# Output products of six experts by seven products of halves instead of eight

## The chip, the cores and the metric

The kernel runs on one NeuronCore of a Trainium2 chip. A core has TensorE (PE, matrix products into the banks of PSUM), VectorE (DVE, elementwise work), ScalarE (ACT, elementwise functions), GpSimd (POOL) and SyncE (SP, which here only issues DMA transfers); each engine works through its own instruction stream, and semaphores order them. PEld in a profile is TensorE's load of the stationary operand, which overlaps its matmuls. The metric is device time in microseconds. Before the change it is 1541.7 us (median of 3 runs, 1541.43 to 1544.1).

## The reference

All arithmetic is float32. Input x is 8 sequences of 256 tokens with 512 features, so 2048 tokens. Two layers follow each other; each has a recurrent attention block (WKV) and a feed-forward block. The feed-forward block of layer 0 is a gated MLP with a Walsh-Hadamard transform; the one of layer 1, which the change touches, is a mixture of eight experts:

```
x = x + tanh(g_xattn[0]) * WKV0(layernorm(x), ctx)
x = x + tanh(g_ffn[0])   * (fwht(silu(n @ W1.T) * (n @ W3.T)) @ W2.T)     # n = layernorm(x)
x = x + tanh(g_xattn[1]) * WKV1(layernorm(x), ctx)
x = x + tanh(g_ffn[1])   * moe(layernorm(x))

def moe(x):                                    # 8 experts, 512 -> 1024 -> 512, two per token
    mult, sel = route(x @ gate_w.T)            # sparsemixer: two experts and two weights per token
    combine = sum over the two of mult * one_hot(sel)
    act = silu(x @ w1[e].T) * (x @ w3[e].T)    # hidden values, 1024 per token
    y[e] = act @ w2[e].T                       # output product, 512 per token
    return sum over e of combine[:, e] * y[e]
```

## The kernel before

**Stages.** The first 880 us or so compute the attention blocks and layer 0's MLP, and send each token's normalised row, with its number and weights, into a queue in DRAM for each of its two experts (`dispatch`, L589). Then come the experts. `EARLY = (6, 7)` are taken first, partly while the last tokens are still being routed; then experts 0 to 5 follow in order (`order`, L1288). The change concerns these six.

**Two parts per expert.** `PARTS` (L40) cuts an expert's tokens in a first part of 256 and a second of up to 336. The second part runs only if the expert has more than 256 tokens: its work stands in `tc.If(needed > 0)` (L1089). For each part, `prepare` (L872) loads the rows of the queue (L893, on SP's queue) and turns them by transposes on TensorE (L865), so that features lie on partitions; `old_rows` (L901) gathers the tokens' present rows of the output by an indirect DMA of POOL into tiles g; `weigh` (L1073) adds weight times y to g; `new_rows` (L910) scatters g back. These transfers go in POOL's queue, and each waits for the one before, because all touch the output.

**First parts** are computed by `compute` (L920). Hidden values come in KC = 8 units of 128, each for all 256 tokens: `hidden` (L718) does four matmuls with W1 and four with W3 (L729, 256 columns), then ScalarE's tanh (L733) and two VectorE operations (L734, L735). Behind unit k follow the output matmuls of unit k-1, one for each block of 128 tokens, 512 columns wide (`add`, L926). So a first part has 2 x 8 of these, and the last ones end it. Between the units a generator of background work, `bg`, is advanced by n = 2 steps (L938): preparing the next parts, `sum_tokens` (L975) and `sum_weights` (L954).

**Second parts** of every expert but 6 are computed by `compute_paired` (L988). There the hidden products already are done by seven products of halves instead of eight (Strassen's scheme in Winograd's form): the features and the hidden units of a weight matrix are each halved, and so are the features and the tokens of the token matrix (HALF = 168). `sum_weights` and `last_sum` (L970) make the sums of the weights' quarters, `sum_tokens` those of the tokens. In each of four rounds k, the products go into three PSUM tiles pa, pb, pc (L1006), VectorE adds them up (L1023 to L1055), and gating gives hidden units k and k+4. The output matmuls of a round are kept in a list `late` and put in between later products by `put` (L1037), for three blocks (128, 128 and 80 tokens), again 8 matmuls of 512 columns each. In the last part of all, `leave` is given: there they come block by block at the end, and each block is weighed and stored as soon as it is done. On TensorE this order is kept as written (`manual_schedule`, L1091).

**Order of work otherwise.** In the expert stage the framework's scheduler orders each engine's instructions by their place in the program and by when their operands and buffers are ready; the order is then fixed for the run. Tiles of one tag share a number of buffers: v4 (4 KB per partition; weights, weight sums, turned tokens) has 35 (L84), u2 16, h1 (256 columns) 17; PSUM has three banks for hidden products (`ps_gl`), three for outputs (`ps_o`) and two for transposes. A new tile waits until a buffer is free. An expert's weights are 12 tiles of 512 KB (8 of W1 and W3, 4 of W2), all loaded from SP's queue by `load_expert` (L846).

**The main loop** (L1304) loads the next expert ahead of a part, then runs the part with its background work:

```
early_load = i or e == order[len(EARLY)]          # L1311
...
if i == 0:
    bg = chain(bg, sum_tokens(f"{e}_1"), sum_weights(e))   # L1320
...
part(e, i, bg, 2, needed, at == len(todo) - 1)    # L1324
```

So the next expert's load stands, in program order, ahead of the second part; for the first of the six, expert 0, it stands ahead of the first part.

Of the kernel before, what the change touches and what calls it, by code (L numbers as in the profile page):

```python
# [8 lines left out]
FP = mybir.dt.float32  # L9
# [8 lines left out]
P = 128  # L18
# [32 lines left out]
def flamingo_kernel(  # L51
# [31 lines left out]
    def v4(name, shape=(P, DC, T)):  # L83
        return work.tile(list(shape), FP, tag="v4", name=name, bufs=35)  # L84
# [19 lines left out]
    def chain(*gens):  # L104
        for gen in gens:
            yield from gen
# [810 lines left out]

    def compute(weights, xq, wt, g, width, name, bg=iter(()), n=0, leave=None):  # L920
        w1, w3, w2 = weights
        blocks = [(b, min(P, width - b * P)) for b in range(len(g))]
        ys = [ps_o.tile([P, D], FP, tag="o", name=f"y_{name}_{b}") for b, _ in blocks]
        ts = []

        def add(k, b, rows):  # L926
            nc.tensor.matmul(  # L927
                ys[b][:rows, :], lhsT=ts[k][:, b * P : b * P + rows], rhs=w2_of(w2, k),
                start=(k == 0), stop=(k == KC - 1),
            )  # L930

        for k in range(KC):
            t = None if width <= T else u2([P, width], f"t_{name}_{k}")
            ts.append(hidden(xq, w1, w3, k, width, f"{name}_{k}", t))
            if k > 0 and leave is None:
                for block in blocks:
                    add(k - 1, *block)
            run(bg, n)  # L938
        for b, rows in blocks:
            for k in range(KC - 1 if leave is None else 0, KC):  # L940
                add(k, b, rows)
            if leave is not None:
                weigh(g[b], ys[b], wt, b, rows)
                leave(b)
        if leave is None:
            for b, rows in blocks:
                weigh(g[b], ys[b], wt, b, rows)

# [37 lines left out]
    def compute_paired(e, tokens, wt, g, name, leave=None):  # L988
        w2 = experts[e][2]
        width = 2 * HALF  # L990
        blocks = [(b, min(P, width - b * P)) for b in range(len(g))]
        ys = [ps_o.tile([P, D], FP, tag="o", name=f"y_{name}_{b}") for b, _ in blocks]
        b11, b21, b22, t1, t2, t3, t4 = tokens
        ts = {}

        def add(k, b, rows):
            nc.tensor.matmul(  # L997
                ys[b][:rows, :], lhsT=ts[k][:, b * P : b * P + rows], rhs=w2_of(w2, k),
                start=(k == 0), stop=(k == KC - 1),
            )  # L1000

        def product(ps, to, k, weights, toks):
            for c in range(2):
                nc.tensor.matmul(  # L1006
                    ps[:, to, :], lhsT=weights[:, c, k * P : (k + 1) * P], rhs=toks[:, c, :],
                    start=(c == 0), stop=(c == 1),
                )

        def twice(t):
            return t.to_broadcast([P, 2, HALF])

        def six(k, n):
            a11, a12, a22, s1, s2, s3, s4 = sums[e][n]
            r = u2([P, 4, HALF], f"h{n}_{name}_{k}")
            ps = ps_gl.tile([P, 3, HALF], FP, tag="gl", name=f"pa{n}_{name}_{k}")
            product(ps, 0, k, a11, b11)
            product(ps, 1, k, a12, b21)
            product(ps, 2, k, s2, t2)  # L1020
            nc.scalar.copy(r[:, 1, :], ps[:, 0, :])

            nc.vector.tensor_tensor(r[:, 0:4:3, :], ps[:, 1:3, :], twice(r[:, 1:2, :]), ALU.add)  # L1023
            yield
            ps = ps_gl.tile([P, 3, HALF], FP, tag="gl", name=f"pb{n}_{name}_{k}")
            product(ps, 0, k, s1, t1)
            product(ps, 1, k, s3, t3)
            product(ps, 2, k, s4, b22)
            nc.vector.tensor_tensor(r[:, 1:3, :], ps[:, 0:2, :], twice(r[:, 3:4, :]), ALU.add)
            nc.vector.tensor_tensor(r[:, 3, :], ps[:, 1, :], r[:, 1, :], ALU.add)  # L1030
            nc.vector.tensor_tensor(r[:, 1, :], ps[:, 2, :], r[:, 1, :], ALU.add)
            yield r


        late = []

        def put(n):  # L1037
            for _ in range(min(n, len(late))):
                add(*late.pop(0))

        for k in range(KC // 2):
            last = k == KC // 2 - 1
            rs = []
            for n in range(2):
                both = six(k, n)
                next(both)
                put(2 * n if not last else 0)
                rs.append(next(both))
            put(2 if not last else 0)
            ps = ps_gl.tile([P, 2, HALF], FP, tag="gl", name=f"pc_{name}_{k}")  # L1050
            for n in range(2):
                product(ps, n, k, sums[e][n][2], t4)
            put(len(late))
            for n in range(2):
                nc.vector.tensor_tensor(rs[n][:, 2, :], ps[:, n, :], rs[n][:, 2, :], ALU.add)  # L1055
            t = u2([P, 4, HALF], f"t_{name}_{k}")
            nc.scalar.activation(t, rs[0], AF.Tanh, scale=0.5)
            nc.vector.scalar_tensor_tensor(rs[0], t, 1.0, rs[0], ALU.add, ALU.mult)
            nc.vector.tensor_tensor(rs[1], rs[0], rs[1], ALU.mult)
            for i, j in enumerate((k, k + 4)):  # L1060
                ts[j] = rs[1][:, 2 * i : 2 * i + 2, :].rearrange("p a t -> p (a t)")
            if leave is None:
                late += [(j, b, rows) for j in (k, k + 4) for b, rows in blocks]
        put(len(late))
        for b, rows in blocks:
            if leave is not None:
                for i in range(KC):
                    add(i // 2 + i % 2 * 4, b, rows)
            weigh(g[b], ys[b], wt, b, rows)
            if leave is not None:  # L1070
                leave(b)

    def weigh(g, y, wt, b, rows):  # L1073
        nc.vector.scalar_tensor_tensor(  # L1074
            g[:rows, :], y[:rows, :], wt[:rows, b : b + 1], g[:rows, :], ALU.mult, ALU.add
        )

    def expert_part(weights, xq, meta, width, name, bg, n, needed=None, last=False):
        who, wt = meta
        blocks = range(-(-width // P))  # L1080
        g = [old_rows(who, b, NT, f"{name}_{b}") for b in blocks]
        if needed is None:
            compute(weights, xq, wt, g, width, name, bg, n)
        else:
            paired = weights in sums
            if paired and weights not in EARLY:
                last_sum(weights)
            done = (lambda b: new_rows(who, b, g[b], NT)) if last else None
            with tc.If(needed > 0):  # L1089
                if paired:  # L1090
                    with tc.manual_schedule(engines={mybir.EngineType.PE}):  # L1091
                        compute_paired(weights, sums[name], wt, g, name, done)
                else:
                    compute(experts[weights], xq, wt, g, width, name, leave=done)
        if not last:
            for b in blocks:
                new_rows(who, b, g[b], NT)
# [120 lines left out]

    def part(e, i, bg, n, needed=None, last=False):
        name = f"{e}_{i}"  # L1220
        expert_part(experts[e] if needed is None else e, parts[name], metas[name], PARTS[i][1], name, bg, n, needed, last)


    n_ps = ps_st.tile([P, NE], FP, tag="st", name="n_all")
# [79 lines left out]
    for at, (e, i) in enumerate(todo):  # L1304
        nxt = order.index(e) + 1

        if nxt == len(EARLY) + 1 and i == 0:
            count_overflow()
            overflow()
        load_next = nxt < NE and order[nxt] not in experts  # L1310
        early_load = i or e == order[len(EARLY)]  # L1311
        if load_next and early_load:
            load_expert(order[nxt])
        needed = None
        if i:
            engines = busy + [mybir.EngineType.Pool] * (at == len(todo) - 1)
            needed = nc.values_load(needs[0:1, e : e + 1], engines=engines, min_val=0, max_val=1)  # L1317
        bg = prepare_on(at)
        if i == 0:
            bg = chain(bg, sum_tokens(f"{e}_1"), sum_weights(e))  # L1320
        elif e == EARLY[0]:

            take(chain(sum_weights(EARLY[1], True), sum_tokens(f"{EARLY[1]}_1")))
        part(e, i, bg, 2, needed, at == len(todo) - 1)  # L1324
        take(bg)

        if load_next and not early_load:
            load_expert(order[nxt])
# [46 lines left out]
```

## Time and profile before

| what | us |
|---|---|
| median of three runs | 1541.7 |
| profiled execution, own time | 1540.96 |
| its span, first to last instruction | 1539.2 |
| TensorE busy (share of the span) | 1488.2 (97%) |
| VectorE busy | 892.5 (58%) |
| ScalarE busy | 285.3 (19%) |
| GpSimd busy | 235.8 (15%) |
| mean granted TensorE clock | 0.984 |

The profile is of one execution; its span leaves out some time before the first and after the last instruction. "Busy" is the time in which an engine works on an instruction; a matmul's end is modelled, so starts are surer than ends. A line such as "L927 PE MATMUL y<-w_e,t" names the code line, the engine, the operation, the tile written and the tiles read; "<-DVE g L1074" after idle time names what ended it. A matmul of float32 operands appears as two TensorE instructions.

### The profile page before, as it was taken

The numbers are of one execution on the slowest core, as the hardware profiler recorded it, in microseconds if no ns is written. First come the engines' busy times: TensorE is split into PE (matmuls) and PEld (weight loads), VectorE is DVE, ScalarE is ACT, GpSimd is POOL, SyncE is SP. The second block draws the span as 40 slices with busy tenths as digits, with TensorE's granted clock in tenths as the row PEclk, the third lists the DMA queues.
The fourth block names the chain that finished last, engine by engine and source line by source line (L and its number), as shares of the span: only waits on it lengthen the run. The fifth ranks groups of instructions, "written<-read, shape, count | busy, mean of one in ns | idle before, by whom it ended". The sixth has DMA issues, their size and how long they took to land. (4 is left out here: it accounts for less than half of the span.)

```text
span 1539.2 us, 18611 instructions
## 1 busy us (share of the span) xinstructions
PE 1488.2 (97%) x7072; PEld 1198.3 (78%) x7072; DVE 892.5 (58%) x1987; ACT 285.3 (19%) x665; POOL 235.8 (15%) x258
## 2 busy tenths in 40 slices
PE   5999999999999999999999799899999999999996
PEld 2988888888888888888877557576877868778693
DVE  6852877978787796976355414353435544355452
ACT  5240313223122322312121100011101111111110
POOL 1100111211121221212112201013101011010110
PEclk9899999999999999999999899999999999999998
DMA  9960001011001101023161305336123151231010
GB/s 335 363 223 14 15 28 42 28 42 42 28 29 41 42 28 44 12 90 117 45 216 49 99 14 182 112 119 217 57 90 126 48 202 52 91 123 33 27 32 17
DMA packets 79494, 135.11 MB, mean 88 GB/s; under 512 B 13084, under 2 KB 26524, under 8 KB 79392
## 3 DMA queue, kind: packets, MB, share of 16 engines
q1 hardware_dynamic: 69280, 108.45, 20.5%
q0 software_dynamic: 8960, 25.25, 4.7%
q8 instruction: 60, 0.98, 0.3%
q14 instruction: 42, 0.34, 0.1%
q10 hardware_dynamic: 1152, 0.09, 0.1%
HBM read 100.05 MB, written 37.90 MB: 90 GB/s over the span
## 5 line engine op out<-in xcount | busy, mean ns | idle before, releaser
L746 PE MATMUL gl_f<-xn,w_a 128*128 128x256 f32 (+1 forms) x1152 | 235.6, 359 | 1.6 <-DVE xn L418 1.6
L746 PE MATMUL gl_f<-xn,w_b 128*128 128x256 f32 (+1 forms) x1152 | 223.9, 356 | 0.0
L746 PEld LDWEIGHTS gl_f<-xn,w_a 128*128 128x128 f32 x1152 | 200.9, 193 | 27.7 <-issue 3.3
L746 PEld LDWEIGHTS gl_f<-xn,w_b 128*128 128x128 f32 x1152 | 199.0, 190 | 23.0
L729 PE MATMUL gl<-q,w_e 128*128 128x256 f32 x768 | 179.4, 386 | 9.6 <-DVEq L1281 6.0
L729 PEld LDWEIGHTS gl<-q,w_e 128*128 128x128 f32 x768 | 146.8, 194 | 45.3 <-issue 27.4
L997 PE MATMUL y<-w_e,h 128*128 128x512 f32 (+1 forms) x288 | 129.5, 592 | 0.0
L911 POOL DMA_INDIRECT out<-g,who_e x40 | 41.7, 1042 | 522.1 <-DVE g L1074 427.9
L818 PE MATMUL o_f<-t_f,w_b 128*128 128x256 f32 x512 | 118.7, 380 | 0.0
L818 PE MATMUL o_f<-t_f,w_a 128*128 128x256 f32 x512 | 117.3, 380 | 0.0
L927 PE MATMUL y<-w_e,t 128*128 128x512 f32 (+1 forms) x240 | 111.0, 592 | 0.0
L818 PEld LDWEIGHTS o_f<-t_f,w_b 128*128 128x128 f32 x512 | 96.2, 190 | 12.5
L818 PEld LDWEIGHTS o_f<-t_f,w_a 128*128 128x128 f32 x512 | 96.2, 190 | 12.5
L753 ACT ACTIVATE t_f<-gl_f 128x256 f32<-128x256 f32 (+1 forms) x144 | 50.1, 360 | 297.3 <-PE gl_f L746 296.8
L755 DVE SCALAR_TENSOR_TENSOR t_f<-t_f,gl_f 128x256 f32<-128x256 f32 (+1 forms) x144 | 53.9, 382 | 80.7 <-ACT t_f L753 80.5
L997 PEld LDWEIGHTS y<-w_e,h 128*128 128x128 f32 (+1 forms) x288 | 49.6, 177 | 54.5 <-issue 54.5
L734 DVE SCALAR_TENSOR_TENSOR t<-t,gl 128x256 f32<-128x256 f32 x48 | 20.2, 421 | 117.4 <-ACT t L733 117.1
L927 PEld LDWEIGHTS y<-w_e,t 128*128 128x128 f32 (+1 forms) x240 | 44.9, 187 | 37.9 <-issue 31.4
L1006 PEld LDWEIGHTS pa<-q,w_e 128*128 128x128 f32 x384 | 57.8, 190 | 8.1 <-issue 7.8
L733 ACT ACTIVATE t<-gl 128x256 f32<-128x256 f32 x48 | 18.5, 385 | 239.0 <-PE gl L729 239.0
L1074 DVE SCALAR_TENSOR_TENSOR g<-y,wt_e,g 128x512 f32<-128x512 f32 (+1 forms) x37 | 27.7, 750 | 60.3 <-PE y L997 44.1
L1006 PE MATMUL pa<-q,w_e 128*128 128x168 f32 x384 | 62.6, 306 | 0.0
(223 smaller groups left out, 2058.6 us busy)
## 6 DMA issues: line engine op xcount, KB each, us to landing
w_e<-in_w1T SPq DMA_DIRECT2D x32, 512.0 KB, 6.6
w_e<-in_w3T SPq DMA_DIRECT2D x32, 512.0 KB, 7.0
w_e<-in_w2T SPq DMA_DIRECT2D x32, 512.0 KB, 11.7
queue<-empty SPq DMA_DIRECT2D x8, 1290.0 KB, 16.5
r<-queue SPq DMA_DIRECT2D x32, 256.0 KB, 4.4
c<-in_ctxT SPq DMA_DIRECT2D x15, 512.0 KB, 3.2
out<-xr SPq DMA_DIRECT2D x16, 256.0 KB, 2.1
x<-in_xT SPq DMA_DIRECT2D x7, 512.0 KB, 3.2
```

The costliest lines, as they stand in the source:

```text
L729: nc.tensor.matmul(ps, lhsT=w13_of(w, c, k), rhs=xn(c)[:, :width], start=(c == 0), stop=(c == DC - 1))
L733: nc.scalar.activation(t, gp, AF.Tanh, scale=0.5)
L734: nc.vector.scalar_tensor_tensor(t, t, 1.0, gp, ALU.add, ALU.mult)
L746: nc.tensor.matmul(ps, lhsT=w13_of(w, c, k), rhs=xn(c)[:, :width], start=(c == 0), stop=(c == DC - 1))
L753: nc.scalar.activation(t, gp, AF.Tanh, scale=0.5)
L755: nc.vector.scalar_tensor_tensor(t, t, 1.0, gp, ALU.add, ALU.mult)
L818: nc.tensor.matmul(o, lhsT=w2_of(w2h[k // KC], k % KC)[:, c * P : (c + 1) * P], rhs=hs[k], start=(k == 0), stop=(k == 2 * KC - 1),)
L911: nc.gpsimd.indirect_dma_start(out=out[:end, :], out_offset=bass.IndirectOffsetOnAxis(ap=who[:, b : b + 1], axis=0), in_=g, in_offset=None ...
L927: nc.tensor.matmul(ys[b][:rows, :], lhsT=ts[k][:, b * P : b * P + rows], rhs=w2_of(w2, k), start=(k == 0), stop=(k == KC - 1),)
L997: nc.tensor.matmul(ys[b][:rows, :], lhsT=ts[k][:, b * P : b * P + rows], rhs=w2_of(w2, k), start=(k == 0), stop=(k == KC - 1),)
L1006: nc.tensor.matmul(ps[:, to, :], lhsT=weights[:, c, k * P : (k + 1) * P], rhs=toks[:, c, :], start=(c == 0), stop=(c == 1),)
L1074: nc.vector.scalar_tensor_tensor(g[:rows, :], y[:rows, :], wt[:rows, b : b + 1], g[:rows, :], ALU.mult, ALU.add)
```

## The change

**Output products of pairs.** A new function, `outputs`, computes y for two blocks of 128 tokens at once. The 1024 hidden units are halved (units 0 to 3, `low`, and 4 to 7, `high`), the 512 outputs are halved (`left`, `right`, HC = 256), and the two blocks of tokens are the third pair of halves. Seven products, each of four accumulating matmuls 256 columns wide, fill the halves of three PSUM banks and one half of a fourth; one ScalarE copy and eight VectorE additions combine them into two SBUF tiles y0 and y1, which are then weighed (the second in two halves). In the last part, each block is scattered as it is done.

**Sums.** `sum_down` makes four sums of quarters of W2 for an expert (eight VectorE operations of 128x512 into four v4 tiles), as the last background work of its first part. `sum_units` makes four sums of hidden units for each k of 0 to 3 (four operations of 128x128 into two h1 tiles), in both parts.

**Where.** First parts of experts 0 to 5 compute their hidden units in the order 0, 4, 1, 5, 2, 6, 3, 7, with no output matmuls in between, and then call `outputs`. Their second parts (`pairs`) do their hidden products without output matmuls in between, then the output matmuls of the third block of 80 tokens as before, then `outputs` for the first two blocks. Experts 6 and 7 are unchanged.

**Around it.** Background work advances by 3 steps per unit instead of 2. Expert 1's load moves from ahead of expert 0's first part to ahead of its second part, like the others. For expert 0 the sums of W1 and W3 come first in the background work.

```
-    def compute(weights, xq, wt, g, width, name, bg=iter(()), n=0, leave=None):
+    def compute(weights, xq, wt, g, width, name, bg=iter(()), n=0, leave=None, e=None):
         w1, w3, w2 = weights
+        if e is not None:
+            hs, ss = {}, {}
+            for k in range(KC // 2):
+                for j in (k, k + KC // 2):
+                    hs[j] = hidden(xq, w1, w3, j, width, f"{name}_{j}")
+                    run(bg, n)
+                ss[k] = sum_units(hs, k, name)
+            return outputs(e, hs, ss, wt, g, name)
...
+    HC = D // 2
+    down = {}
+
+    def sum_down(e):
+        w2 = experts[e][2]
+        t1, t2, t3, t4 = (v4(f"t{i}_2_{e}", (P, 4, HC)) for i in (1, 2, 3, 4))
+        down[e] = t1, t2, t3, t4
+        for i in range(2):
+            ks = slice(2 * i, 2 * i + 2)
+            (b11, b12), (b21, b22) = ((w2[j][:, :, :HC], w2[j][:, :, HC:]) for j in (i, i + 2))
+            for t, a, b in ((t1, b12, b11), (t2, b22, t1[:, ks, :]), (t3, b22, b12), (t4, t2[:, ks, :], b21)):
+                nc.vector.tensor_tensor(t[:, ks, :], a, b, ALU.subtract)
+                yield
+
+    def sum_units(hs, k, name):
+        (a11, a21), (a12, a22) = ((hs[j][:, :P], hs[j][:, P : 2 * P]) for j in (k, k + KC // 2))
+        s1, s2, s3, s4 = (
+            t[:, i, :] for t in (h1(2 * P, f"{n}_{name}_{k}").rearrange("p (i t) -> p i t", i=2) for n in ("sa", "sb"))
+            for i in range(2)
+        )
+        nc.vector.tensor_tensor(s1, a21, a22, ALU.add)
+        nc.vector.tensor_tensor(s2, s1, a11, ALU.subtract)
+        nc.vector.tensor_tensor(s3, a11, a21, ALU.subtract)
+        nc.vector.tensor_tensor(s4, a12, s2, ALU.subtract)
+        return s1, s2, s3, s4
+
+    def outputs(e, hs, ss, wt, g, name, leave=None):
...
+        def product_of(ps, cs, a, b):
+            for k in range(KC // 2):
+                nc.tensor.matmul(ps[:, cs], lhsT=a(k), rhs=b(k), start=(k == 0), stop=(k == KC // 2 - 1))
...
+        u, y0, y1 = (u2([P, D], f"{n}_{name}") for n in ("u", "y0", "y1"))
+        ps = bank("a")
+        product_of(ps, left, unit_of(low, 0), weight_of(low, left))
+        product_of(ps, right, unit_of(high, 0), weight_of(high, left))
+        nc.scalar.copy(u[:, left], ps[:, left])
+        nc.vector.tensor_tensor(y0[:, left], ps[:, right], u[:, left], ALU.add)
+        ps = bank("b")
+        product_of(ps, left, sum_of(2), lambda k: t2[:, k, :])
+        product_of(ps, right, sum_of(1), lambda k: t1[:, k, :])
+        nc.vector.tensor_tensor(u[:, right], ps[:, left], u[:, left], ALU.add)
+        nc.vector.tensor_tensor(y0[:, right], ps[:, right], u[:, right], ALU.add)
+        nc.vector.tensor_tensor(y1[:, right], ps[:, right], u[:, right], ALU.add)
+        ps = bank("c")
+        product_of(ps, left, sum_of(4), weight_of(high, right))
+        product_of(ps, right, sum_of(3), lambda k: t3[:, k, :])
+        nc.vector.tensor_tensor(y0[:, right], ps[:, left], y0[:, right], ALU.add)
+        weigh(g[0], y0, wt, 0, P)
+        if leave is not None:
+            leave(0)
+        nc.vector.tensor_tensor(u[:, left], ps[:, right], u[:, right], ALU.add)
+        nc.vector.tensor_tensor(y1[:, right], ps[:, right], y1[:, right], ALU.add)
+        ps = bank("d")
+        product_of(ps, left, unit_of(high, 1), lambda k: t4[:, k, :])
+        weigh(g[1][:, right], y1[:, right], wt, 1, P)
+        nc.vector.tensor_tensor(y1[:, left], u[:, left], ps[:, left], ALU.subtract)
+        weigh(g[1][:, left], y1[:, left], wt, 1, P)
+        if leave is not None:
+            leave(1)
...
     def compute_paired(e, tokens, wt, g, name, leave=None):
+        pairs = e in down
+        if pairs:
+            blocks = blocks[2:]
...
+        def held(k):
+            return pairs or k == KC // 2 - 1
...
-                put(2 * n if not last else 0)
+                put(2 * n if not held(k) else 0)
...
-            put(len(late))
+            put(len(late) if not pairs else 0)
...
+            if pairs:
+                ss[k] = sum_units(ts, k, name)
+            if leave is None or pairs:
                 late += [(j, b, rows) for j in (k, k + 4) for b, rows in blocks]
         put(len(late))
...
+        if pairs:
+            outputs(e, ts, ss, wt, g, name, leave)
...
-        early_load = i or e == order[len(EARLY)]
+        early_load = i > 0
...
         if i == 0:
-            bg = chain(bg, sum_tokens(f"{e}_1"), sum_weights(e))
+            if e == order[len(EARLY)]:
+                bg = chain(sum_weights(e), bg, sum_tokens(f"{e}_1"), sum_down(e))
+            else:
+                bg = chain(bg, sum_tokens(f"{e}_1"), sum_weights(e), sum_down(e))
...
-        part(e, i, bg, 2, needed, at == len(todo) - 1)
+        part(e, i, bg, 3, needed, at == len(todo) - 1)
```

More of the change, by code (lines that the diff above doesn't have):

```diff
@@ new lines, in outputs, with unit_of, weight_of, sum_of @@
+    def outputs(e, hs, ss, wt, g, name, leave=None):
+        w2 = experts[e][2]
+        t1, t2, t3, t4 = down[e]
+        left, right = slice(0, HC), slice(HC, D)
+        low, high = (lambda k: k), (lambda k: k + KC // 2)
+        def unit_of(half, at):
+            return lambda k: hs[half(k)][:, at * P : (at + 1) * P]
+        def weight_of(half, cs):
+            return lambda k: w2_of(w2, half(k))[:, cs]
+        def sum_of(i):
+            return lambda k: ss[k][i - 1]
+        def product_of(ps, cs, a, b):
+            for k in range(KC // 2):
+                nc.tensor.matmul(ps[:, cs], lhsT=a(k), rhs=b(k), start=(k == 0), stop=(k == KC // 2 - 1))
+        def bank(n):
+            return ps_o.tile([P, D], FP, tag="o", name=f"y{n}_{name}")
+        u, y0, y1 = (u2([P, D], f"{n}_{name}") for n in ("u", "y0", "y1"))
[26 more added lines that the diff above has]
+            leave(1)
@@ L991, in compute_paired @@
         blocks = [(b, min(P, width - b * P)) for b in range(len(g))]
-        ys = [ps_o.tile([P, D], FP, tag="o", name=f"y_{name}_{b}") for b, _ in blocks]
+        pairs = e in down
+        if pairs:
+            blocks = blocks[2:]
+        ys = {b: ps_o.tile([P, D], FP, tag="o", name=f"y_{name}_{b}") for b, _ in blocks}
         b11, b21, b22, t1, t2, t3, t4 = tokens
-        ts = {}
+        ts, ss = {}, {}
         def add(k, b, rows):
@@ L1041, in compute_paired @@
         for k in range(KC // 2):
-            last = k == KC // 2 - 1
             rs = []
@@ L1046, in compute_paired @@
                 next(both)
-                put(2 * n if not last else 0)
+                put(2 * n if not held(k) else 0)
                 rs.append(next(both))
-            put(2 if not last else 0)
+            put(2 if not held(k) else 0)
             ps = ps_gl.tile([P, 2, HALF], FP, tag="gl", name=f"pc_{name}_{k}")
@@ L1061, in compute_paired @@
                 ts[j] = rs[1][:, 2 * i : 2 * i + 2, :].rearrange("p a t -> p (a t)")
-            if leave is None:
+            if pairs:
+                ss[k] = sum_units(ts, k, name)
+            if leave is None or pairs:
                 late += [(j, b, rows) for j in (k, k + 4) for b, rows in blocks]
@@ L1065, in compute_paired @@
         for b, rows in blocks:
-            if leave is not None:
+            if leave is not None and not pairs:
                 for i in range(KC):
@@ L1076, in weigh, with expert_part @@
         )
-    def expert_part(weights, xq, meta, width, name, bg, n, needed=None, last=False):
+    def expert_part(weights, xq, meta, width, name, bg, n, needed=None, last=False, e=None):
         who, wt = meta
@@ L1082, in expert_part @@
         if needed is None:
-            compute(weights, xq, wt, g, width, name, bg, n)
+            compute(weights, xq, wt, g, width, name, bg, n, e=e)
         else:
@@ L1220, in part @@
         name = f"{e}_{i}"
-        expert_part(experts[e] if needed is None else e, parts[name], metas[name], PARTS[i][1], name, bg, n, needed, last)
+        expert_part(experts[e] if needed is None else e, parts[name], metas[name], PARTS[i][1], name, bg, n, needed, last, e if needed is None else None)
     n_ps = ps_st.tile([P, NE], FP, tag="st", name="n_all")
```

## The prediction

> **What bounds the kernel now.** I read the page first, then the expert stage alone: its stages as windows, its chain of waits in order of time, VectorE's timeline, and last the queues. The page says that TensorE is the bound of the whole.
>
> ```profile
> span 1539.2 us, 18611 instructions
> ...
> PE 1488.2 (97%) x7072; PEld 1198.3 (78%) x7072; DVE 892.5 (58%) x1987; ACT 285.3 (19%) x665; POOL 235.8 (15%) x258
> ```
>
> The two halves of one expert say it more sharply. These are stages of expert 2: columns are length, then busy time and instruction count of PE, PE's weight loads, VectorE, ScalarE, GpSimd, then granted clock and DMA share.
>
> ```profile
> 1143.90:1187.40 43.50, 43.50 (x182) 32.18 (x181) 19.38 (x30) 5.95 (x16) 4.96 (x5) 1.00 0.50 178
> 1187.40:1239.90 52.50, 52.50 (x273) 40.46 (x273) 24.57 (x51) 5.46 (x12) 5.72 (x6) 1.00 0.13 42
> ```
>
> TensorE is busy for all of both stages, at the full clock; VectorE is busy for 19.4 of 43.5 us and 24.6 of 52.5 us. So here a TensorE instruction that goes away shortens the run by its own length, as long as nothing new makes TensorE wait. The chain in order of time (start, length, what) gives the prices:
>
> ```profile
> 1143.86 6.91 PE gl L729 x32
> 1150.76 1.72 PE y L927 x4
> ...
> 1180.49 3.45 PE gl L729 x16
> 1183.94 3.43 PE y L927 x8
> ...
> 1229.60 10.30 PE y L997 x24
> ```
>
> Every matmul of the program is two TensorE instructions here (eight units of 8 matmuls are 128 instructions). A 128x256 matmul costs 3.45/8 = 0.431 us, a 128x512 one 10.30/12 = 0.858 us. Twice the first is 0.862: width is paid almost exactly in proportion.
>
> How many pairs run? Second parts are conditional. Rows by shape of the expert stage:
>
> ```profile
> L997 PE MATMUL y<-w_e,h 128*80 128x512 f32 x96 | 47.9, 592 | 0.0
> ```
>
> A paired second part has 8 matmuls of its 80-row block, 16 instructions; 96 are six parts. Expert 7 is one. Expert 0's second part is skipped: its outputs end at 1041.2 and expert 1's hidden units begin at 1043.3 with nothing between. So the change acts on six first parts and five second parts: **11 pairs of blocks**, not 12.
>
> **The change part by part.**
>
> *Matmuls removed and added.* A pair costs 16 x 0.858 = 13.73 us now and 7 x 4 = 28 half-width matmuls, 28 x 0.4315 = 12.08 us, after: 1.65 us less. Ten pairs (the eleventh is the kernel's end, below): **-16.5 us**. [...] The row of this kernel decides, as the same width with a fresh weight load each time runs in the hidden units: 0.431.
>
> *The kernel's end.* The last part (expert 5's second) stores each block as it is done. Now its last weigh begins at 1527.18 and its scatter at 1528.20. Hidden work ends near 1506.4; after it 8 matmuls of the third block (6.87), then 12.08: TensorE ends 1525.3, 1.65 earlier. But blocks 0 and 1 now finish 1.7 us apart, not 6.9, and a scatter waits for the one before:
>
> ```profile
> 1431.33 1.01 POOL L911 DMA_INDIRECT out<-g,who_e  x1 [40.79 <-DVE g L1074]
> 1434.89 0.98 POOL L911 DMA_INDIRECT out<-g,who_e  x1 [2.55 <-DMA out<-g,who_e]
> ...
> 1528.20 0.97 POOL L911 DMA_INDIRECT out<-g,who_e  x1 [5.88 <-DVE g L1074]
> ```
>
> 1434.89 - 1431.33 = 3.56 us from one to the next. Block 0's product ends at 1523.6, add 0.45 and weigh 0.75, scatter at 1525.1; block 1's at about 1528.6 instead of 1528.2. So this pair gives **+0.4 us**.
>
> *VectorE, first parts.* This is the price of the change. Rows:
>
> ```profile
> 1158.46 1.22 DVE L960 TENSOR_TENSOR s<-w_e,w_e 128x1024 f32<-128x1024 f32 x1
> 1159.71 1.23 DVE L962 TENSOR_TENSOR s<-s,w_e 128x1024 f32<-128x1024 f32 x1
> ...
> 1191.38 0.33 DVE L1030 TENSOR_TENSOR h<-pb,h 128x168 f32<-128x168 f32 x1
> 1191.74 0.33 DVE L1031 TENSOR_TENSOR h<-pb,h 128x168 f32<-128x168 f32 x1
> ...
> 1195.41 0.56 DVE L1055 TENSOR_TENSOR h<-pc,h 128x168 f32<-128x168 f32 x2
> ```
>
> A sum of 1024 columns is 1.22 us; 336 columns are 0.51, 168 are 0.33, so I estimate 0.69 for 512 and 0.29 for 128. Start to start they are shorter (0.36 for a dependent pair of 168; the two of L1055 take 0.56 together): about 0.62 and 0.26. Per first part the change adds 8 sums of W2 (5.0 us) and 16 sums of units (4.2). Already there: eight gatings of 0.80 (6.4), token sums 1.9, sums of W1 and W3 7.1, small ones 0.7. Together 25.3 us, while hidden work on TensorE lasts 8 x 3.45 + 2.1 of transposes = 29.7. Formerly output matmuls stretched this to 41 us.
>
> What TensorE needs at the junction, counted from T, the end of the hidden work: the last unit at T + 1.73 + 3 x 0.43 = T+3.0 (it is ready 1.3 us after its last matmul: 1183.94 to 1185.27), the last unit sums at T + 3.45 + 1.29 = T+4.75. Behind a late sum wait, on TensorE, the remaining output products and the whole second part. Whether VectorE is done by then hangs on when its background sums may begin. Now they begin at 1158.46, 14.6 us into the part, though VectorE had idled before: behind the transposes of the next tokens. From 15 us there would be 4.0 of gating, 7.1, 5.0 and three groups of unit sums 3.15: 19.3, so done at 34.3 us = T+4.6, and the sum needed half a microsecond before its end: just in time. Three background steps per unit instead of two bring the transposes earlier (I take 12 to 13 us, an estimate), which leaves 2 us to spare. [...] Ends: no stall; 2.5 us in each of six first parts (15 us). I take 0.4 each, near the lower end because the estimate closes: **+2.4 us**.
>
> *VectorE, second parts.* A round k takes 7.99 us of TensorE (28 x 2 instructions at 0.143); VectorE has 5.6 and gets 1.05 of unit sums. Outputs no longer stand between rounds, as they don't between rounds 0 and 1 now, where TensorE doesn't pause. At the end the third block's 6.87 us of matmuls hide the last gating (3.0) and sums. Nothing, and without that cover about 1 us each.
>
> *Banks and last operations.* Of three output banks, the fourth product group needs the first one's, read 9 us before. Combining a pair takes VectorE eight additions of 256 columns (0.42 each by the gating's row of that width) and weighing 0.75 + 2 x 0.42, together 5 us beside 12.1 us of products. After the last product about 1.8 us are left instead of 0.8; its first work in the second part is due 2.1 us in. Nothing there; at the skipped part of expert 0, where expert 1 starts cold, between 0 and 1: **+0.5 us**.
>
> *Buffers and queues.* Tiles of 4 KB have 35 buffers. While expert e+1 is loaded there live 12 of e, 6 sums, 3 of tokens, 12 of e+1 and one spent: 34 now, 38 with four W2 sums. When the spent one is free, the last two W2 tiles of e+1 (1 MB) must wait for e's second part. They are first used 15 us or more into the next part, after the sums of W1 and W3. Behind them on SP's queue wait the loads of queue rows, which now run ahead during the second part; a load has landed 4 to 12 us after issue, and the transposes stand 9.5 us in. I take 0; up to 2 us each time. Expert 1's load moves behind expert 0's first part on SP's queue, though its buffers are free: it was issued from 990 on, and should be by 1020, needed at 1043: 0, else about 10 once. ScalarE's copy per pair (0.39) and the gathers, some 14 us early, are covered.
>
> Sum: -16.5 + 0.4 + 2.4 + 0.5 = **-13.2 us**. The profiled execution took 1540.96 us, 1.8 beyond its span and 0.7 below the median, 1541.7. I carry the difference over to the median: **1528.5 us**.
>
> **The rivals.**
> - *VectorE ends late.* Its background sums begin 16 to 18 us into first parts. For it: today's 14.6, and little slack. Against: output matmuls no longer stand before the transposes. Stalls of 1 to 2 us, six times: 1534 to 1539; I say 1536.
> - *Weights come late* (slower). W2's sums take buffers on which the loads of w1 and w3 of the next expert then wait, not just two W2 tiles, until the second part ends. The loads now start at the first part's very beginning:
>
> ```profile
> 1144.25 0.98 SPq L241 DMA_DIRECT2D w_e<-in_w1T  x2
> ```
>
> and TensorE would stand for about 2 us of issue and 7 of landing at each of five experts: +45, about 1574. It turns the result from 2.7 us per expert on. Against: 10 buffers are free without waiting.
> - *Expert 1's load alone is late*: +10, about 1538.
> [...]
>
> **How the numbers follow.** Main case 0.62 (own range 1525 to 1533), VectorE late 0.17, weights late 0.10, expert 1 alone 0.08, others 0.03. A measurement tells 0.2% (3.1 us) from no change. Faster: 0.62 + 0.14 + 0.06 = 0.82; same 0.05; slower 0.13. The range leaves out the slow case, the worst stalls and a few hundredths below: 1524 to 1539.
>
> **What would show it.** First parts near 41.9 us instead of 43.5; half-width output matmuls at 0.43 each; second parts near 50.9 us; PE idle before the second to fourth bank under 1 us per part. Wrong if: the chain shows VectorE or a load ahead of output matmuls in each expert; hidden units wait for w1; half-width output matmuls are dearer than 0.45.

## The result, and the profile after

The changed kernel takes **1525.12 us** (median of 4 runs, 1523.93 to 1526.1) beside 1542.9 for the kernel before (median of 4, 1541.43 to 1544.57): a ratio of 0.9884 with the interval 0.9867 to 0.9901, that is 15 to 21 us less. The forecast was 1528.5 in 1524 to 1539; the result lies at the lower edge of the range of its main case, 1525 to 1533. The profiled execution took 1526.1 us, with a span of 1524.2.

The page's head after the change:

```profile
span 1524.2 us, 19432 instructions
...
PE 1470.5 (96%) x7336; PEld 1248.7 (82%) x7336; DVE 984.6 (65%) x2310; ACT 288.5 (19%) x676; POOL 237.5 (16%) x258
```

TensorE is still the bound, with 264 more instructions in 17.7 us less busy time: 11 pairs with 24 more instructions each, so the count of pairs was right. VectorE gained 323 operations and 92 us.

The stages of expert 2 (length; busy time and count of PE, PE's weight loads, VectorE, ScalarE, GpSimd; granted clock; DMA share, GB/s):

```profile
1138.93:1180.92 41.99, 41.99 (x206) 36.68 (x205) 29.64 (x64) 6.29 (x17) 6.29 (x5) 1.00 0.56 195
1180.92:1231.79 50.87, 50.87 (x297) 45.00 (x296) 30.33 (x77) 5.82 (x13) 5.22 (x5) 1.00 0.11 35
```

The first part fell from 43.50 to 41.99 us and the second from 52.50 to 50.87: forecast were 41.9 and 50.9. TensorE is busy for the whole of both, at the full clock.

The chain in order of time, from the end of the first part's hidden units on:

```profile
1152.04 16.84 PE gl L729 x78
1168.88 3.02 PE ya L1004 x14
1171.90 0.43 PE yb L1004 x2
1172.33 0.55 PE ya L1004 x2
1172.88 3.02 PE yb L1004 x14
1175.90 3.45 PE yc L1004 x16
1179.35 1.73 PE yd L1004 x8
1181.08 1.71 PE pa L1100 x12
```

L1004 is the matmul of `product_of`. Sixteen instructions, eight half-width matmuls, take 3.45 us: 0.431 each, as in the hidden units. The third line of the outputs shows all that is left of the junction: the last unit's own matmul is put behind one of the second bank and takes 0.55 instead of 0.43, 0.12 us.

To see where the time went I cut each execution in four: TensorE's wait at the jump behind the overflow experts, just ahead of expert 0; the first parts of experts 0 and 1, with the skipped second part of expert 0 between them; everything from expert 1's second part to TensorE's end (four first and five second parts); and what follows TensorE's end. Each kernel has two traces, the second from the experiments below.

| us | before | before, again | after | after, again | mean difference |
|---|---|---|---|---|---|
| up to the jump | 989.93 | 994.18 | 992.12 | 990.96 | -0.5 |
| wait at the jump | 6.04 | 5.90 | 3.89 | 4.07 | -2.0 |
| first parts of 0 and 1 | 95.20 | 94.83 | 92.04 | 91.07 | -3.5 |
| from expert 1's second part on | 435.97 | 435.96 | 421.60 | 421.60 | -14.4 |
| behind TensorE's end | 12.06 | 12.13 | 14.55 | 14.60 | +2.5 |
| span | 1539.2 | 1543.0 | 1524.2 | 1522.3 | -17.9 |

The fourth row repeats to 0.01 us, and it holds most of the gain: 4 first parts at -1.53 and 5 second parts at -1.65 are -14.4. The rest is what the experiments had to explain.

### The profile page after: what moved, and what is told of

It is laid out like the page before. It is cut to its first block, busy times and chain, and to the rows that moved or that the text cites. A ratio compares the mean times of both kernels' runs of the same rounds, so it can differ in the third digit from the quotient of the medians.

```text
span 1524.2 us, 19432 instructions
## 1 busy us (share of the span) xinstructions
PE 1470.5 (96%) x7336; PEld 1248.7 (82%) x7336; DVE 984.6 (65%) x2310; ACT 288.5 (19%) x676; POOL 237.5 (16%) x258
## 5 line engine op out<-in xcount | busy, mean ns | idle before, releaser
L729 PE MATMUL gl<-q,w_e 128*128 128x256 f32 x768 | 174.0, 385 | 8.2 <-DVEq L1382 3.9
L729 PEld LDWEIGHTS gl<-q,w_e 128*128 128x128 f32 x768 | 146.4, 193 | 29.4 <-issue 8.5
L746 PE MATMUL gl<-q,w_e 128*128 128x256 f32 x256 | 59.2, 384 | 0.0
L746 PEld LDWEIGHTS gl<-q,w_e 128*128 128x128 f32 x256 | 49.1, 193 | 11.3 <-issue 5.3
L1091 PE MATMUL y<-w_e,h 128*80 128x512 f32 (+1 forms) x128 | 56.9, 592 | 0.0
L903 POOL DMA_INDIRECT g<-out,who_e x40 | 45.5, 1138 | 62.7 <-DMA out<-g,who_e 30.3
L757 DVE TENSOR_TENSOR t_f<-t_f,gl_f 128x256 f32<-128x256 f32 (+1 forms) x144 | 53.7, 381 | 0.7
L460 DVE RECIPROCAL e<-e 128x512 f32<-128x512 f32 (+1 forms) x18 | 53.9, 2992 | 0.1
```

The source lines that it names most:

```text
L460: nc.vector.reciprocal(den, den)
L729: nc.tensor.matmul(ps, lhsT=w13_of(w, c, k), rhs=xn(c)[:, :width], start=(c == 0), stop=(c == DC - 1))
L746: nc.tensor.matmul(ps, lhsT=w13_of(w, c, k), rhs=xn(c)[:, :width], start=(c == 0), stop=(c == DC - 1))
L757: nc.vector.tensor_tensor(t, t, lp, ALU.mult)
L903: nc.gpsimd.indirect_dma_start(out=g, out_offset=None, in_=out[:end, :], in_offset=bass.IndirectOffsetOnAxis(ap=who[:, b : b + 1], axis=0) ...
L1091: nc.tensor.matmul(ys[b][:rows, :], lhsT=ts[k][:, b * P : b * P + rows], rhs=w2_of(w2, k), start=(k == 0), stop=(k == KC - 1),)
```

## The experiments

**The two halves of the change, and its order alone.** Four kernels, run beside one set of runs of the kernel before (30 runs, median 1542.9). The first is the changed kernel, once more.

> The changed kernel itself, once more, so that the parts below are measured beside it. If the 17.8 us between the two medians is right, it lies 17 to 18.5 us below the kernel before; if the traced executions are (spans 15.0 us apart), about 15. The price of the matmuls alone gives -16.5 for ten pairs plus what the end costs, about -15.7.

It took 1525.47 us, 0.9891 [0.9877, 0.9905] of before.

Second parts with eight products again:

```
-        pairs = e in down
+        pairs = False
```

> Second parts compute their first two blocks in eight products again; the six first parts keep theirs in seven, and all sums of W2, the order of loads and three background steps per unit stay. Theory (each pair is worth its matmuls, 13.73 - 12.08 = 1.65 us, as VectorE is just in time): 6 x -1.65 = -9.9, with 0.1 us of waiting each about -9.3 against the kernel before; the end keeps its old form, last scatter 1.2 us behind TensorE. Rival (part of the gain comes from the moved loads and the order of background work, not from matmuls): -11 to -13. Rival (waits in the first parts eat gain): -6 or less.

It took **1527.51** us, 0.9908 [0.9894, 0.9922]: -15.4, far more than the 9.9 us of its matmuls, and more than the rival had.

First parts with eight products again, everything else as changed:

```
-        expert_part(..., needed, last, e if needed is None else None)
+        expert_part(..., needed, last, None)
```

> First parts compute their blocks in eight products again; the five second parts keep seven. Theory: four pairs at -1.65 = -6.6, and the kernel's end, where 1.65 us less of TensorE meets a last scatter that now comes 3.67 us after TensorE's end instead of 1.23: +0.8; together -5.8 against the kernel before. First and second alone add up to the whole, about -15. Rival (order and loads give a gain of their own): -8 to -9, and the two parts alone add up to 2 to 3 us more than the whole.

It took **1538.14** us, 0.9971 [0.9961, 0.9982]: -4.8. So the parts alone do not add up to the whole: -15.4 and -4.8 exceed the -17.4 by 2.8 us. That is the excess that the rival had, but not its -8 to -9.

No pair and no sums of W2; both edits above, and

```
-                bg = chain(sum_weights(e), bg, sum_tokens(f"{e}_1"), sum_down(e))
+                bg = chain(sum_weights(e), bg, sum_tokens(f"{e}_1"))
...
-                bg = chain(bg, sum_tokens(f"{e}_1"), sum_weights(e), sum_down(e))
+                bg = chain(bg, sum_tokens(f"{e}_1"), sum_weights(e))
```

> No pair in seven products and no sums of W2: what is left of the change is three background steps per unit, expert 1's load after expert 0's first part, and its sums of weights ahead of other background work. Theory: 0 against the kernel before, within 1 us, since TensorE does the same matmuls and each load was early. Rival (the order gives the 2 us by which the measured gain exceeds the price of the matmuls): -2 to -3. Rival (load or first expert suffers): +1 or more.

It took **1544.31** us, 1.0013 [1.0006, 1.0021]: 1.4 us slower, so the last of the three guesses was right. And the kernel before, traced a second time:

> The kernel before, unchanged, once more with its own trace: how much two executions of the same instructions differ, and where. The medians of before and after lie 17.5 us apart and the two traced executions 15.0. Theory (the stages from the start of expert 1's second part on are the same in every execution, and the differences come from the waits and the half clock around experts 0 and 1): 435.97 us from there to TensorE's end within 0.1, and if the execution is longer than the first one (its median is 1.9 us above it), the excess lies ahead of that point, in longer waits or a longer stretch at half clock. Rival (the clock or the matmuls themselves differ between executions): the 435.97 us change in proportion, by 0.5 us or more.

It took 1543.88 us, 1.0 [0.999, 1.001]; its traced span is 1543.0, 3.8 above the first one's. The theory held: 435.96 us from expert 1's second part on. The excess lies even ahead of the jump (994.18 instead of 989.93). One trace of a kernel can thus be 2 us off its median, and the one on which the forecast was built was: the two traced executions gave -15.0, the means of two traces each -17.9.

The stages of these runs, from the same rows of TensorE's timeline ("jump" is the wait there):

| us | jump | parts 0 and 1 | from expert 1's second part on | behind | span | median |
|---|---|---|---|---|---|---|
| first parts only | 3.77 | 89.41 | 429.83 | 12.14 | 1525.8 | 1527.51 |
| second parts only | 3.79 | 96.49 | 427.77 | 14.55 | 1535.1 | 1538.14 |
| order only | 3.93 | 100.56 | 435.97 | 12.19 | 1544.8 | 1544.31 |

The column from expert 1's second part on is as the price of the matmuls has it, and it adds up: first parts give -6.14 (4 x -1.53), second parts -8.20 (5 x -1.64), the order 0.00, together -14.34 of the -14.37 measured. What doesn't add up lies ahead of it.

*The jump.* In all twelve traces of kernels that load expert 1 later, TensorE waits 3.8 to 4.1 us there; in the two of the kernel before, 5.9 and 6.0. TensorE's rows at the start of expert 0, before and with the order alone:

```profile
995.97 8.58 PE L729 MATMUL gl<-q,w_e 128*128 128x256 f32 x32 [6.04 <-DVEq L1281]
```

```profile
996.08 10.08 PE L729 MATMUL gl<-q,w_e 128*128 128x256 f32 x32 [3.93 <-DVEq L1382]
```

The releaser is VectorE's queue at the end of the conditional around the overflow experts. Since the order alone shows it, it belongs to the moved load or the other edits of order and not to the pairs, and it is counted in each of the parts: two of the 2.8 us by which they exceed the whole. The traces show where the time goes: VectorE needs 5.1 and 5.0 us from its branch at the end of the conditional to the semaphore that releases TensorE in the two traces of before, 2.9 after and 3.0 with the order alone, with no operation in between. Which of the order's edits does it is not shown. During this passage the kernel before is loading expert 1 (DMA share 0.79 from 990 to 996, against 0.13 after), so the moved load is the likely one, but no run moves it alone.

*Expert 0.* With the order alone, and with pairs in second parts only, expert 0's output matmuls stand between its units, and now wait for the gating on VectorE, which sums of weights precede. These two rows are of the order alone:

```profile
1006.92 1.98 PE L935 MATMUL y<-w_e,t 128*128 128x512 f32 x4 [0.75 <-DVE t L735]
...
1013.97 1.98 PE L935 MATMUL y<-w_e,t 128*128 128x512 f32 x4 [1.61 <-DVE t L735]
```

With second parts only they are 2.38 and 2.06. With the order alone parts 0 and 1 take 5.5 us more than before (100.56 against 95.0 in the mean); these two waits are 2.4 of them, longer waits at the skipped part 1.3, and more half clock behind the jump 1.5. Where first parts are paired and no sum is doubled, these waits are gone or under 1 us, because outputs come after all units. So with the new order, pairing the first parts is worth more than its matmuls: it pays back what the order costs. Stage by stage, first parts alone, against the mean of the two traces of before: -1.4 ahead of the jump, -2.2 at it, -5.6 in parts 0 and 1 (3.06 of matmuls, 2.5 of waits and half clock, of which half clock is the larger part: no stretch of it follows the skipped part here), -6.1 after them, +0.0 at the end: -15.3. Second parts alone: +0.4, -2.2, +1.5, -8.2, +2.5: -6.0.

*The clock.* TensorE restarts twice here: after the jump and after the skipped part. There its first matmuls mostly ran at half the clock, for a stretch that differs from trace to trace (see the last section). Windows of 6.8 us before, and of 3.4 us after and with first parts only, from the first matmul of expert 1 (granted clock third from last):

```profile
1043.30:1050.10 6.80, 5.37 (x12) 3.84 (x13) 0.00 (x0) 0.00 (x0) 0.98 (x1) 0.50 0.61 198
1050.10:1056.90 6.80, 6.80 (x29) 5.22 (x29) 1.68 (x4) 0.77 (x2) 3.26 (x4) 1.00 0.89 294
```

```profile
1044.30:1047.70 3.40, 3.40 (x9) 2.65 (x10) 0.17 (x2) 0.00 (x0) 0.98 (x1) 0.53 1.03 351
1047.70:1051.10 3.40, 3.40 (x17) 3.01 (x16) 0.84 (x2) 0.38 (x1) 0.00 (x0) 0.97 0.89 287
```

```profile
1041.80:1045.20 3.40, 3.40 (x16) 3.01 (x17) 0.16 (x1) 0.00 (x0) 0.98 (x1) 1.00 0.78 227
```

After, 9 instructions fit into 3.4 us where 16 or 17 do at the full clock. A stretch of 3.4 us costs 1.7, one of 6.8 up to 3.4. PE's busy time doesn't show it: it is 3.40 of 3.40 in both. The stage of the two first parts then is the sum of its work (2 x 41.99 = 83.98 with pairs), its waits and these: with first parts only, 2.69 of waiting and 2.7 that the first unit behind the jump takes longer than one at full clock give 89.4, as measured; after, 0.93 + 3.42 of waiting and 1.7 + 1.7 give 91.7, of 92.04. In the same way the missing stretch behind the skipped part flatters the trace of first parts only by about 1.7 us.

**VectorE's slack.** The trace after shows VectorE's operations around the end of a first part's hidden units; TensorE's output matmuls start at 1168.7:

```profile
1169.11 1.22 DVE L1062 TENSOR_TENSOR w_e<-w_e,w_e 128x1024 f32<-128x1024 f32 x1
1170.24 0.42 DVE L734 SCALAR_TENSOR_TENSOR t<-t,gl 128x256 f32<-128x256 f32 x1
1170.57 1.22 DVE L1062 TENSOR_TENSOR w_e<-w_e,w_e 128x1024 f32<-128x1024 f32 x1
1171.71 0.42 DVE L735 TENSOR_TENSOR t<-t,gl 128x256 f32<-128x256 f32 x1
1172.16 0.29 DVE L981 TENSOR_TENSOR sa<-t,t 128x128 f32<-128x128 f32 x1
1172.37 0.28 DVE L983 TENSOR_TENSOR sb<-t 128x128 f32<-128x128 f32 x1
1172.57 0.28 DVE L982 TENSOR_TENSOR sa<-sa,t 128x128 f32<-128x128 f32 x1
1172.89 0.29 DVE L984 TENSOR_TENSOR sb<-t,sa 128x128 f32<-128x128 f32 x1
```

VectorE hardly pauses from 12 us into the part to here, and the last unit's sums end 4.5 us behind the end of hidden work, where 4.75 had been worked out as the deadline. I read this as just in time, and tried it with more work: four and then eight of the sums of W2 done twice (the kernel before has 1544.38 beside these runs).

```
-                nc.vector.tensor_tensor(t[:, ks, :], a, b, ALU.subtract)
+                for _ in range(1 + i):                  # eight: range(2)
+                    nc.vector.tensor_tensor(t[:, ks, :], a, b, ALU.subtract)
```

> Four of the eight sums of W2 are done twice, with the same result: four more VectorE sums of 512 columns, about 0.6 us each, 2.4 us in each of six first parts. Theory (VectorE ends just in time for the last sums of units, so its time is now TensorE's): nearly all of it shows, 1.5 to 2.4 us per first part, +9 to +14 us against the changed kernel, with PE waiting on the last unit's gating or its sums. Rival (VectorE is busy 65% of the time and has slack): 0.

> All eight sums of W2 are done twice: 4.9 us more of VectorE in each first part. Theory: +2.4 us per first part over the run with four, so +24 to +28 us against the changed kernel, more than the whole change gives; if the two last operations of background work then fall behind the last unit's sums, about 2.4 us of each part are hidden and it is +12 to +16. Rival (slack): 0 to 5.

They took **1524.93** us (0.9882 [0.9865, 0.9898]) and **1528.8** (0.9904 [0.9887, 0.9922]). That is nothing, and 3.3 to 3.7 us more than the changed kernel's two medians. From expert 1's second part on they take 421.55 and 423.50 us, against 421.60: nothing, and 1.9 us in four first parts. My theory fell, by its own numbers; the rival of slack, 0 and 0 to 5, came true. The lines of both traces show why. With eight doubled, the end of the same stage on TensorE:

```profile
1168.34 3.19 PE L1005 MATMUL ya<-w_e,t 128*128 128x256 f32 x14
1171.36 1.82 PE L1005 MATMUL yb<-t,sa 128*128 128x256 f32 x6
1173.02 1.46 PE L1005 MATMUL yc<-w_e,sb 128*128 128x256 f32 x6
1174.31 0.59 PE L1005 MATMUL ya<-w_e,t 128*128 128x256 f32 x2
1174.95 2.43 PE L1005 MATMUL yb<-t,sa 128*128 128x256 f32 x10
```

and with four doubled, where VectorE's L1063 is the L1062 of before:

```profile
1168.11 0.28 DVE L982 TENSOR_TENSOR sa<-t,t 128x128 f32<-128x128 f32 x1
...
1169.32 2.35 DVE L1063 TENSOR_TENSOR w_e<-w_e,w_e 128x1024 f32<-128x1024 f32 x2
```

With four more sums the scheduler puts the two last sums of weights, 2.3 us which nobody needs yet (they belong to the second part), behind the last unit's sums: as much as was added. With eight, 2.5 us remain, and TensorE takes the products of the three ready units from three banks first (14, 6 and 6 instructions) before it asks for the last unit: 0.55 us is lost here of 2.5 (as much in experts 3 and 4, 0.2 in expert 5). Expert 0's first part has less to spare: there TensorE waited 0.41 us (four doubled) and 1.60 us (eight doubled) for the last unit's gating, against none after. A densely packed engine is no engine at its limit, while some of what it does can go later.

The other question was whether the late start of background work matters. Sums of W1 and W3 come first for all six experts:

```
-            if e == order[len(EARLY)]:
+            if True:
```

> For all six experts the sums of W1 and W3 come first in the background work, ahead of the transposes of the next tokens, as the change has it for expert 1 alone. Theory (VectorE is in time, by little): the sums start at the part's begin and VectorE is done several us earlier, but TensorE only wins back its waits of 0.1 us per first part: 0 to -0.6 against the changed kernel. If transposes then come late for the next part, slower by 1 or more.

> Sums of W1 and W3 first in the background work, and all eight sums of W2 done twice. Theory (what limits VectorE is when its background work may start, not how much there is): the 4.9 us of added work fit into the time that VectorE idled at the part's begin, 0 to +3 us against the changed kernel. Rival (amount of VectorE work in the part is the limit): the same loss as with the doubled sums alone.

They took **1524.28** us (0.9867 [0.9848, 0.9885]) and **1526.9** (0.9890 [0.9874, 0.9907]). From expert 1's second part on: 420.68 and 421.46 us. A first part is 41.75 us with weights first, 0.24 less than after, and 42.01 with all eight sums doubled, where the doubled sums alone have 42.54. The direction was as expected, and 0.24 us is more than the 0.1 that was expected of it: an early start takes back the 0.12 us at the junction and as much in the units, and half a microsecond of what doubling costs; but it was a matter of a quarter of a microsecond per part, not of the 4.9 us that I had thought at stake.

**The end.** The third bank holds only the product that block 0 still lacks, and the one with the third sum goes into the fourth:

```
         product_of(ps, left, sum_of(4), weight_of(high, right))
-        product_of(ps, right, sum_of(3), lambda k: t3[:, k, :])
         nc.vector.tensor_tensor(y0[:, right], ps[:, left], y0[:, right], ALU.add)
         weigh(g[0], y0, wt, 0, P)
...
         ps = bank("d")
+        product_of(ps, right, sum_of(3), lambda k: t3[:, k, :])
         product_of(ps, left, unit_of(high, 1), lambda k: t4[:, k, :])
```

> The third bank of a pair holds only the product that block 0 still lacks; the product with the third sum moves into the fourth bank. So block 0 is weighed and stored 4 x 0.43 = 1.73 us of TensorE earlier, with as many matmuls in all. Theory (at the kernel's end the last scatter waits for the scatter before it, 3.5 us from one to the next): last scatter about 1.9 us after TensorE's end instead of 3.67, kernel 1.7 us faster than the changed one, nothing anywhere else. Rival (the last combination on VectorE becomes longer, as two halves now come out of the last bank): 0 or slower by up to 1.

It took **1523.69** us, 0.9868 [0.9848, 0.9889]. GpSimd's last two scatters after, and with this edit:

```profile
1509.66 0.98 POOL L911 DMA_INDIRECT out<-g,who_e  x1 [10.02 <-DVE g L1175]
1513.16 0.98 POOL L911 DMA_INDIRECT out<-g,who_e  x1 [2.52 <-DMA out<-g,who_e]
```

```profile
1506.49 0.98 POOL L911 DMA_INDIRECT out<-g,who_e  x1 [8.09 <-DVE g L1175]
1510.60 0.97 POOL L911 DMA_INDIRECT out<-g,who_e  x1 [3.13 <-DVE g L1175]
```

After, the last scatter waits for the one before it (released by a DMA, 3.50 us from start to start). With the edit it waits for VectorE's last weighing, 2.2 us behind TensorE's end (1508.42): the time from TensorE's end to the end of the span falls from 14.55 to 13.18, 1.4 us of the 1.7 expected, since both halves of block 1 now come out of the last bank.

**Both of these together:**

> Sums of weights first for all experts and block 0 stored earlier, together: the sum of what the two give alone, -1.7 to -2.3 us against the changed kernel.

It took **1523.0** us, 0.9869 [0.9849, 0.9889] of the kernel before and the lowest of all. Its stage from expert 1's second part on is 420.68 and what follows is 13.26: 2.2 us less than after by the trace, about what the two give alone. In whole runs that is at the edge of what can be told (1525.12 and 1525.47 for the changed kernel).

**Fewer buffers.**

```
-        return work.tile(list(shape), FP, tag="v4", name=name, bufs=35)
+        return work.tile(list(shape), FP, tag="v4", name=name, bufs=33)
```

> 33 instead of 35 buffers of 4 KB: four instead of two W2 tiles of the next expert have to wait until the second part gives buffers back. Theory (these tiles and the queue's loads behind them are hidden): 0 against the changed kernel, within 1 us. Rival (late weights bound the next part, as in the slower case of the prediction): +2 us or more at each of five experts, +10.

It took **1526.85** us, 0.9891 [0.9872, 0.9910]; from expert 1's second part on 421.54 us, against 421.60. The median is 1.4 to 1.7 us above those of the changed kernel, measured beside other runs, and the intervals overlap; the stage in which late weights would show has none of it. SyncE's queue after, and with 33 buffers:

```profile
1149.50 82.86 SPq L249 DMA_DIRECT2D w_e<-in_w2T  x4
1232.45 2.80 SPq L893 DMA_DIRECT2D r<-queue  x5
```

```profile
1150.56 19.52 SPq L241 DMA_DIRECT2D w_e<-in_w3T  x2
1206.43 27.76 SPq L249 DMA_DIRECT2D w_e<-in_w2T  x4
1234.29 2.91 SPq L893 DMA_DIRECT2D r<-queue  x5
```

A row here merges issues that lie far apart. After, the four W2 tiles are issued at 1149.50, 1168.91, 1205.62 and 1231.98 (the second part begins at 1180.92), so two wait for the second part. With 33 buffers they go at 1206.43, 1232.79, 1233.21 and 1233.72, and one of w3 waits until 1169.71. The loads of queue rows still come behind them, at the next part's start, and TensorE waits for none of it.

## Why the prediction was right, and where it wasn't

- **Matmuls, -16.5: right.** Half-width output matmuls take 0.431 us, as the row of the hidden units had it, and first and second parts fell by 1.53 and 1.65.
- **The kernel's end, +0.4: mechanism right, size off.** The chain of two scatters came as forecast, 3.50 us apart (3.56 forecast). The time behind TensorE's end grew by 2.5, so with its 1.64 us of matmuls the pair gave +0.8. Block 0's scatter started with TensorE's end, not 0.2 ahead of it, as an addition for block 1 went before its weighing; the rest, about 0.2, may be how a matmul's modelled end is read.
- **VectorE in first parts, +2.4: too dear.** Background sums began 14 us in, not 12 to 13, and the last unit's sums ended at T + 4.5, a quarter of a microsecond ahead of the deadline; yet TensorE lost 0.12 us at a junction, which would be 0.7 in six. The wrong step was to count VectorE's work as one block with a deadline: 2.3 us of it (the last sums of weights) can go behind the deadline, and TensorE has other products to do first, as the doubled sums showed. The price of a sum of 128 columns, estimated at 0.26 us from start to start, was about right: in the lines above, those that do not need the one just before them start 0.20 to 0.21 us after it, though each lasts 0.28 to 0.29; the one that does starts 0.32 behind.
- **Second parts, 0: right**, to 0.01 us.
- **The skipped part of expert 0, +0.5: not seen.** The two first parts fell by 3.5 us, of which their matmuls are 3.06. Two traces of the changed kernel differ by 1 us there, 0.93 of it one wait for gating, so half a microsecond can't be told.
- **Buffers, 0: right.** The last two W2 tiles waited for the second part and the queue's rows behind them, as forecast, and cost nothing. With four waiting it was the same.
- **Expert 1's load, 0 or +10: a gain was overlooked.** It was in time, so the 0 held for what it priced. But the step looked only at whether the load comes late, not at what it may have been in the way of: without it, or without what else moved with it, the wait at the jump is 2.0 us shorter.
- **Carrying the difference over to the median.** With more runs the median of before is 1542.9 and not 1541.7, and the trace of before was an execution 1.9 us under it: its difference to one trace of after is 15.0, where the medians have 17.4 to 17.8.

In terms of the sum: -13.2 became -17.9 in the traces (means of two each). So the matmuls carried the forecast, and what it missed was a gain that it had not looked for and two allowances for losses that hardly came. 2.0 are the jump, 1.7 VectorE's unneeded allowance, 0.9 the skipped part's, 0.5 lies ahead of the jump and is chance, and the end takes 0.4 back.

Of the rivals, late weights were the one to fear, and the run with 33 buffers shows no start of it. VectorE was not late in experts 2 to 5: even with 4.9 us more work in each first part TensorE lost only 0.2 to 0.6 us there. In expert 0's it then waited 1.60 us.

## What to carry to other kernels

Where an engine is busy for a whole stage, take the price of a change from the nearest row of the same width, and look at the stages alone: that from expert 1's second part on repeated to 0.01 us where the two traces of the kernel before differed by 3.8. Before calling another engine just in time, ask which of its operations could go later, and double some of its work to see. Output work that comes after all units, instead of between them, no longer waits for each unit's gating. Where gating came late, as in expert 0 with the new order (waits of 2.4 and 4.4 us), that was worth more than the fewer matmuls (1.53); in experts 2 to 5, where it was in time, it was worth nothing.

## What the hardware did that I had not expected

- **Half clock after a wait.** At the two restarts around expert 0 the granted clock was 0.50 for 6.83 us each in the trace of before and for 3.41 us each in that of after. Behind the jump half clock shows in all fourteen traces: the first 32 instructions of expert 0 took 8.58 to 10.08 us, or the first 48 took 12.28 to 13.63, where later rows at the full clock have 7.14 and 10.53. Behind the skipped part it shows in ten (in four of them the first 44 instructions of expert 1 took 11.42 us, where three of the other traces have 9.73 or 9.74). There waits of 3.42, 3.37 and 2.10 us were followed by it, and ones of 2.69, 2.60, 3.26 and 3.39 were not, so the length of the wait alone doesn't decide. In the traces of before and after, the changes of the granted clock lie whole multiples of 3.41 us apart, and each stretch of that length from 100 us on has 1.00 or 0.50 throughout. The full-clock stretches that half clock followed are those in which TensorE stood for 1.55 us or more; in those that the full clock followed it stood for 1.19 us at most. A half-clock stretch was followed by another one where it stood for 1.37 us or more, and by the full clock where it stood for 0.51 or less. So before, the wait of 2.10 us lay almost whole in one stretch (2.09 us), and half clock followed. After, the 3.89 us at the jump were parted: full clock followed the stretch with 1.18 us of standing, and half clock the next, with 2.70.
- **TensorE stood for 2 to 6 us at each of two jumps.** It stood 3.8 to 6.0 us at the end of one conditional, until VectorE's queue had passed; that wait was shorter in every kernel that no longer loads an expert at that time (3.8 to 4.1 against 5.9 and 6.0). At the skipped part it stood 1.9 to 3.5 us, mostly until VectorE had passed its own branch and made a small operation behind it (L855), and in the three traces of before and of the order alone another 0.9 to 2.5 us a few matmuls later.
